# A four-layer convolution kernel: h2 of a first chunk kept in SBUF, a projection of two bands at once, and x2 stored less its group's mean

## The chip, the cores and the metric

The program runs on one core of a Trainium2 chip, in fp32 throughout. The metric is device time in microseconds. All engines work from queues of their own: PE multiplies matrices (PEld loads its weights), DVE, ACT and POOL work on 128 partitions elementwise, SP and the others issue DMAs, and instructions wait for one another by semaphores.

## What is computed

The input x is [4, 384, 64, 64]: batch B = 4, channels C = 384, which the kernel holds as three chunks (j = 0, 1, 2) of 128 partitions. Four residual layers follow each other, each on the group-normalized input:

```python
x = x + L0(gn(x))   # attention on 96 channels, then a 384 x 384 projection
x = x + L1(gn(x))   # 384 x 384, an 8 x 8 block filter, a 3 x 3 depthwise convolution,
                    # g = gelu(t[:, :192]) * t[:, 192:], then w_out: 192 -> 384
x = x + L2(gn(x))   # 3 x 3 and 5 x 5 depthwise convolutions, gates, a channel mixer
                    # h1 = gelu(bn(w1 tok)): 384 -> 768, h2 = bn(w2 h1): 768 -> 384
x = x + L3(gn(x))
```

Layer 3 is a 7 x 7 depthwise convolution whose kernel depends on the image; with v = gn(x2):

```python
x_w = gelu(mean(v) @ w_avg.T + b_avg + max(v) @ w_max.T + b_max)
xr = x_w * w_mix                                  # [b, c, 7, 7]
Gx = sqrt(sum(xr * xr)); Nx = Gx / (mean_c(Gx) + eps)
kern = gamma * (xr * Nx) + beta                   # depthwise, zero padding of 3
```

So kern is a factor per (b, c) times w_mix plus a constant beta: the kernel computes the convolution with w_mix (the same for all images) and a 7 x 7 box sum, and combines them with the factors a_s and b_s when they are known.

## The kernel before

**Attention beside layer 1.** For each batch the attention runs in 64 steps. A step's scores are four matmuls with 32 rows (L715), then the exponentials (ACT, L723) and the products with v (PE, L752). Beside the steps of batch b, the generator of layer 1 for batch b - 1 is drawn on by `side_by_side`, in shares of cost that each `yield` states. The last batch's layer 1 runs alone. Layer 1 works in eight bands of eight image rows: each column tile of a band is multiplied, filtered and brought back, then the 3 x 3 taps give three accumulators acc[0..2] (192 gated channels remain: 128 in acc[1], 64 in partitions 64 to 127 of acc[2]). `band_out` projects one band, three band heights behind: per output chunk one matmul with 128 rows (L965), one with 64 (L966) into the same PSUM tile, and a DVE add to the residual (L969). What stands in the queue of an engine is settled when the program is built, by a scheduler that takes what is ready in order of emission, and what is marked `high_priority` ahead of it.

**Layers 2 and its mixer.** Depthwise convolutions are matmuls with strips: `z_` holds all channels of a chunk transposed (rows of the image along the partitions), `toep` are band matrices that DVE and POOL build as products (L1137, L1744). The F stage (3700 to 4194 us) computes h2 = w2 h1 per batch and block of 1024 columns, copies it out of PSUM (ACT, L1439), takes its statistics (DVE, L1440) and stores it to DRAM (POOL's queue), for all j. The batch norm's scale and shift (gh, g0) are known only after all batches. `z_` (128 x 17412 fp32) stands unused during F.

**Layer 3 (`phase_g`, from about 4195 us).** `x2_of(j, b)` loads h2 in quarters of 1024 columns, scales it into PSUM (ACT, L1688, 512 columns each), adds it to the residual x (DVE, L1691), takes the sum of squares (ACT, L1693) and the maximum (DVE, L1694), and stores x2. For j = 0, `to_strips` normalizes a third of the image into `y` (ACT, L1710), transposes it on PE (L1720) and copies it into `z` (ACT L1727, DVE L1725), one batch behind `x2_of`. For j = 1 and 2 x2 is read again from DRAM and `half_strips` does the same (L1649, L1653, L1658, L1660); the scales must be laid out for two half-chunks, which `pair_scales` does by small DMAs (L1628).

`conv7` convolves eight channels: it loads a piece of w_mix (L1735), builds four `toep` (L1744, every third on POOL), and runs 32 matmuls (L1757) into PSUM. For j = 0 and 1 the result goes to DRAM (`raw`, L1766); for j = 2 the rest is added (L1769) and the output is stored. Beside the convolutions of j = 0, x2 for j = 1 and 2 is computed; then `factors` gives a_s and b_s; `boxes` (L1788 to L1851) forms the 7 x 7 box sums of each x2, combines x2, the box sum and, for j < 2, the raw convolution (L1837, L1847), and stores the output.

In this version x2 stands as it is: the group's mean gm enters where it is read, as a bias in L1649 and L1710, as the fill value and as the offsets -7 gm and -6 gm of the box sums (L1793, L1812 to L1823). The padding of the normalized image is zero, so the padding of x2 would be gm.

Of the kernel before, what the change touches and what calls it, by code (L numbers as in the profile page):

```python
# [21 lines left out]
F32 = mybir.dt.float32  # L22
# [138 lines left out]
def _layout(i):  # L161
# [38 lines left out]
    w_out_t[64:, 1] = w_out[P:]  # L200
# [26 lines left out]
class _Builder:  # L227
# [301 lines left out]
    def side_by_side(self, b, steps, others):  # L529

        per_step = ((176 if b else 0) + (42 if b + 1 < B else 0)) / 64
        ahead = 0.0
        for n, _ in enumerate(steps):
            while others is not None and ahead < n * per_step:
                piece = next(others, None)
                if piece is None:
                    others = None
                else:
                    ahead += piece
        for _ in others or ():  # L540
            pass
# [255 lines left out]
    def layer1(self, b):  # L797
# [9 lines left out]
        for n in range(-2, 4 * 11):  # L807
# [35 lines left out]
            if w == 0 and h > 2:  # L843
                k = h - 3
                yield from self.band_out(b, acc.pop(k), k, st)
# [80 lines left out]
    def band_taps(self, h, alone, acc):  # L926
# [9 lines left out]
        for j in range(NJ):  # L936
            acc.append(self.wk("acc", "acc", 5))
# [16 lines left out]
            if j == 2:  # L954
                nc.scalar.activation(acc[0][64:P], acc[2][0:64], AF.Gelu)
                nc.vector.tensor_mul(acc[2][64:P], acc[2][64:P], acc[0][64:P])
            yield

    def band_out(self, b, acc, h, st):

        nc = self.nc
        x = self.block("xa_out", self.xa[b], h, "xo", 2)
        for o in range(NJ):
            m = self.pa("out_m1") if b == B - 1 else self.pm("out_m")
            nc.tensor.matmul(m, lhsT=self.w_out[:, 0, o * P : (o + 1) * P], rhs=acc[1], start=True, stop=False)  # L965
            nc.tensor.matmul(  # L966
                m, lhsT=self.w_out[64:P, 1, o * P : (o + 1) * P], rhs=acc[2][64:P], start=False, stop=True
            )
            nc.vector.tensor_add(x[:, o], x[:, o], m)  # L969
            yield 2.0  # L970
        self.stats(st, x, h)
        nc.gpsimd.dma_start(self.x1[b][:, :, h * 512 : (h + 1) * 512], x)
# [5 lines left out]
    def open_strips(self, ctx):  # L978

        pool = ctx.enter_context(self.tc.tile_pool(name="strips", bufs=1, side="right"))  # L980
# [3 lines left out]
        self.nc.gpsimd.memset(self.z_[:, P * 132 : P * 132 + 4], 0.0)  # L984

# [317 lines left out]
    def phase_ef(self, strips):  # L1303
        tc, nc = self.tc, self.nc
        with ExitStack() as ctx:
# [110 lines left out]
            for b in range(B):  # L1416
                for i in range(4):
# [9 lines left out]
                    for j in range(NJ):  # L1427
                        out = io.tile([P, 1024], F32, tag="x", name="f_h2")
# [12 lines left out]
                        nc.gpsimd.dma_start(self.h2[b][:, j, blk], out)  # L1441
# [18 lines left out]
    def phase_g(self):  # L1460
# [8 lines left out]
        with ExitStack() as ctx:  # L1469
# [26 lines left out]
            self.s_s, self.s_b = (cp.tile([P, NJ, B], F32, tag=k, name=k) for k in ("s_s", "s_b"))  # L1496
            self.a_pair = cp.tile([P, NJ, 2, 2, 2], F32, tag="a_pair", name="a_pair")

            self.gm = cp.tile([P, NJ, B], F32, tag="gm", name="gm")
            self.off = cp.tile([P, NJ, B, 3], F32, tag="off", name="off")  # L1500
# [3 lines left out]
            self.z = self.z_[:, 0 : P * 136].rearrange("p (c k b) -> p c k b", k=34, b=B)  # L1504
            nc.gpsimd.memset(self.z_[:, P * 136 :], 0.0)
            nc.gpsimd.memset(self.z[:, :, 0], 0.0)
            self.group_means()
            behind = iter(())
            for b in range(B):
                for x in self.x2_of(0, b):  # L1510
                    next(behind, None)
                for _ in behind:
                    pass
                behind = self.to_strips(0, b, x)
            for _ in behind:
                pass
            self.pair_scales(1)
# [10 lines left out]
            for j in range(NJ):  # L1528
# [12 lines left out]
                if j == 0:  # L1541
# [3 lines left out]
                    self.pair_scales(2)  # L1545
# [5 lines left out]
    def group_means(self):  # L1551
# [4 lines left out]
        for i, k in enumerate((-6.0, -7.0, 2.0)):  # L1556
            nc.vector.tensor_scalar(self.off[:, :, :, i], self.gm, k, None, ALU.mult)
        nc.gpsimd.memset(self.s_s, 1.0)
        nc.vector.tensor_scalar(self.s_b, self.gm, -1.0, None, ALU.mult)
# [12 lines left out]
    def factors(self):  # L1572
# [3 lines left out]
        d, avg, mx = tile_of("g_d"), tile_of("g_avg"), tile_of("g_max")  # L1576
        nc.vector.tensor_sub(avg, self.mean2, self.gm)
# [9 lines left out]
        nc.vector.tensor_sub(mx, mx, self.gm)  # L1587
# [32 lines left out]
        nc.vector.tensor_copy(self.s_s[:, 2], self.a_s[:, 2])  # L1620
        nc.vector.scalar_tensor_tensor(self.s_b[:, 2], self.gm[:, 2], -1.0, self.a_s[:, 2], ALU.mult, ALU.mult)

    def pair_scales(self, j):

        for half in range(2):
            for u in range(2):
                for k, v in enumerate((self.s_s, self.s_b)):
                    self.nc.gpsimd.dma_start(  # L1628
                        self.a_pair[64 * u : 64 * u + 64, j, k, half],
                        v[64 * half : 64 * half + 64, j, u::2],  # L1630
                    )

    def half_strips(self, j, half):

        nc = self.nc
        for pair in range(2):
            for part in range(3):
# [10 lines left out]
                s, b = (self.a_pair[:, j, k, half, pair : pair + 1] for k in range(2))  # L1648
                nc.scalar.activation(y[:, inside], y[:, inside], AF.Identity, bias=b, scale=s)  # L1649
                for i, (k0, n) in enumerate(((0, 4), (4, 4), (8, 3))):  # L1650
# [6 lines left out]
                    if i == 1:  # L1657
                        nc.vector.tensor_copy(zv.rearrange("p c k b -> p k b c"), mv)  # L1658
                    else:
                        nc.scalar.copy(zv, mv.rearrange("p k b c -> p c k b"))  # L1660
# [10 lines left out]
    def x2_of(self, j, b):  # L1671

        nc = self.nc
# [6 lines left out]
        for q in range(4):  # L1680
            sl = slice(q * 1024, (q + 1) * 1024)

            h = self.gw_p.tile([P, 1024], F32, tag="w7", name="g_h2", bufs=3)
            nc.sync.dma_start(h, self.h2[b][:, j, sl])
            for v in range(2):
                m = self.pm("x2_m")
                part = slice(q * 1024 + v * 512, q * 1024 + v * 512 + 512)
                nc.scalar.activation(  # L1688
                    m, h[:, v * 512 : v * 512 + 512], AF.Identity, bias=at(self.g0), scale=at(self.gh)
                )  # L1690
                nc.vector.tensor_add(x[:, part], x[:, part], m)  # L1691
# [3 lines left out]
            yield None  # L1695
# [3 lines left out]
    def to_strips(self, j, b, x):  # L1699
# [3 lines left out]
        for part in range(3):  # L1703
            y = self.gt_p.tile([P, 11 * P], F32, tag="y", name="ax2", bufs=2)
            lo, hi = (22 * part - 1) * W, (22 * part + 21) * W
            if part == 0:
                nc.gpsimd.memset(y[:, 0:W], 0.0)
            if part == 2:
                nc.gpsimd.memset(y[:, N - lo :], 0.0)
            nc.scalar.activation(  # L1710
                y[:, max(lo, 0) - lo : min(hi, N) - lo],
                x[:, max(lo, 0) : min(hi, N)],
                AF.Identity,
                bias=self.s_b[:, j, b : b + 1],
                scale=self.s_s[:, j, b : b + 1],
            )
            for i, (k0, n) in enumerate(((0, 4), (4, 4), (8, 3))):
                m = self.pm("strip_m")
                for k in range(n):
# [166 lines left out]
```

## Time and profile before

| | us |
|---|---|
| median of 3 runs (4963.12 to 4970.23) | 4968.51 |
| the profiled execution | 4966.63 |
| its span in the profile, mean clock 0.962 | 4964.9 |
| attention, beside layer 1 of the batch before | 0 to about 2270 |
| layer 1 of the last batch alone | to about 2540 |
| layer 2's convolutions | 2543 to 3180 |
| mixer, first product | 3200 to 3690 |
| mixer, second product (F) | 3700 to 4194 |
| layer 3: head, until its first convolution matmul | 4195 to 4289 |
| layer 3: j = 0, and x2 of j = 1, 2 | 4289 to 4490 |
| layer 3: j = 1, 2 and the boxes | 4490 to 4965 |

The profile is that of one execution. A row of the groups gives line, engine, operation, result and operands with the tile's form and the number of instructions; then busy time, mean duration of one in ns, and the engine's idle time ahead of them with what ended it. A matmul in fp32 counts twice, since it runs in two passes. In the page's second part each digit is a fortieth of the span. In tables by stretch, the columns are the engines' busy time (and number of instructions), the granted clock of PE, the DMA engines' busy share, and GB/s.

### The profile page before, as it was taken

Reading aid. Unit: us, or ns where it says so; the run is one execution under the profiler, and the core shown is the slowest. Engines: PE = TensorE matmul, PEld = TensorE weight load, DVE = VectorE, ACT = ScalarE, POOL = GpSimd, SP = SyncE. Lnnn points to the kernel's source line nnn. Section 1 sums busy time; section 2 is a strip of 40 time slices with the busy share of each in tenths; the row PEclk is TensorE's granted clock in tenths of the full one; section 3 lists DMA queues with packets and bytes.
Section 4 is the critical chain, followed back from the end, with each engine's and each line's share of the span. In section 5 each row is a group of like instructions: output and inputs, shape, how many; then the busy total and the mean of one; then the engine's idle time right before and its main releaser. Section 6 shows DMA issues by size and latency. Waiting matters only on the chain.

```text
span 4964.9 us, 47732 instructions
## 1 busy us (share of the span) xinstructions
PE 4552.7 (92%) x17665; PEld 2564.5 (52%) x17665; DVE 2769.8 (56%) x4438; ACT 2136.4 (43%) x2873; POOL 777.5 (16%) x593
## 2 busy tenths in 40 slices
PE   5999999999999999998989999699999998677988
PEld 2343444434443344444557888444444443577888
DVE  5322465644666445555867778655531112667898
ACT  4444344454444444444435666411123333764321
POOL 1000000000000000000025555100000001125554
PEclk9999999999999999998989999799999999699999
DMA  5210211211111111112338999776664443896776
GB/s 169 73 47 30 85 54 55 72 56 39 64 64 51 55 45 58 58 57 78 120 122 276 291 292 292 250 278 256 256 245 157 153 152 132 316 343 203 239 255 227
DMA packets 346710, 752.64 MB, mean 152 GB/s; under 512 B 22779, under 2 KB 173158, under 8 KB 337510
## 3 DMA queue, kind: packets, MB, share of 16 engines
q1 hardware_dynamic: 280728, 475.46, 30.1%
q0 software_dynamic: 32640, 151.28, 7.9%
q10 hardware_dynamic: 33102, 122.77, 6.3%
q8 instruction: 143, 2.34, 0.2%
q14 instruction: 97, 0.79, 0.0%
HBM read 447.16 MB, written 302.25 MB: 151 GB/s over the span
## 4 chain that ended last, share of the span: by engine, by line
PE 45%; DVE 9%; DMA 4%; ACT 3%; issue 3%; POOL 1%; SPq 0%; ACTq 0%; DVEq 0%; POOLq 0%
PE h_s L1380 10%; PE h_m L1432 10%; PE conv_m L1156 9%; PE av L752 3%; PE t_m L871 2%; PE conv_m L1757 2%; DVE acc L948 2%; DMA wmix<-in_mix_t 1%; DMA g_h<-h 1%; PE out_m L966 1%; PE proj_m L785 1%; PE sc_s L715 1%; DVE toep L1744 1%; PE taps_m L941 1%; DVE toep L1137 1%
## 5 line engine op out<-in xcount | busy, mean ns | idle before, releaser
L752 PE MATMUL av<-probs,vt 128*128 128x512 f32 x2048 | 965.6, 607 | 0.0
L723 ACT ACTIVATE probs<-sc_s 128x1024 f32<-128x1024 f32 x512 | 500.9, 1021 | 789.8 <-PE av L752 783.7
L752 PEld LDWEIGHTS av<-probs,vt 128*128 128x128 f32 x2048 | 371.7, 192 | 468.1 <-issue 461.0
L1156 PE MATMUL conv_m<-toep,z 128*128 128x256 f32 x2304 | 519.4, 385 | 10.6 <-DVE toep L1137 5.1
L948 DVE SCALAR_TENSOR_TENSOR acc<-band,vecs,acc 128x512 f32<-128x512 f32 x708 | 496.9, 747 | 45.7 <-POOL band L909 39.9
L1432 PE MATMUL h_m<-f_h,cm_w_t 128*128 128x512 f32 x1152 | 496.7, 595 | 8.7 <-ACT f_h L1422 8.7
L1156 PEld LDWEIGHTS conv_m<-toep,z 128*128 128x128 f32 x2304 | 439.4, 193 | 71.0 <-DVE z L1089 4.9
L1757 PE MATMUL conv_m<-toep,z 128*128 128x128 f32 x3072 | 392.8, 286 | 42.1 <-DVE toep L1744 19.2
L1757 PEld LDWEIGHTS conv_m<-toep,z 128*128 128x128 f32 x3072 | 378.7, 202 | 44.4 <-POOL toep L1744 18.2
L1380 PE MATMUL h_s<-e_tok,cm_w_t 128*128 128x512 f32 x768 | 363.4, 596 | 5.5 <-DVE e_tok L1365 5.5
L1137 POOL TENSOR_TENSOR toep<-w,band 128x1536 f32<-128x1536 f32 x94 | 324.0, 3447 | 278.0 <-PE conv_m L1156 232.0
L1432 PEld LDWEIGHTS h_m<-f_h,cm_w_t 128*128 128x128 f32 x1152 | 220.0, 191 | 285.4 <-issue 273.3
L715 PE MATMUL sc_s<-q,k 32*128 32x512 f32 x2048 | 296.3, 647 | 21.9 <-ACT probs L723 21.4
L1440 DVE BATCH_NORM_STATS2 h_st<-f_h 128x6 f32<-128x512 f32 x96 | 66.4, 694 | 429.1 <-ACT f_h L1439 429.1
L871 PE MATMUL t_m<-w_in_t,xb 128*128 128x384 f32 x768 | 276.7, 495 | 3.4 <-DVE coef L888 2.1
L1387 ACT COPY e_h<-h_s 128x1024 f32<-128x1024 f32 x96 | 97.2, 1012 | 401.5 <-PE h_s L1380 401.5
L785 PE MATMUL proj_m<-xm,w_proj_t 128*128 128x512 f32 x576 | 265.2, 599 | 4.6 <-DVE xm L738 3.5
L792 DVE SCALAR_TENSOR_TENSOR x_res<-proj_m,bn_c,x_res 128x512 f32<-128x512 f32 x96 | 71.8, 748 | 319.0 <-PE proj_m L785 315.9
L1380 PEld LDWEIGHTS h_s<-e_tok,cm_w_t 128*128 128x128 f32 x768 | 147.0, 192 | 189.5 <-issue 183.2
L1389 DVE BATCH_NORM_STATS2 h_st<-e_h 128x6 f32<-128x512 f32 x192 | 123.4, 685 | 202.8 <-ACT e_h L1387 202.8
L871 PEld LDWEIGHTS t_m<-w_in_t,xb 128*128 128x128 f32 x768 | 142.9, 192 | 139.0 <-issue 59.3
L1380 PE MATMUL h_s<-z,cm_w_t 128*128 128x512 f32 x384 | 196.2, 593 | 0.0
(380 smaller groups left out, 6206.2 us busy)
## 6 DMA issues: line engine op xcount, KB each, us to landing
d<-d_o ACTq DMA_DIRECT2D x96, 512.0 KB
c_d<-d SPq DMA_DIRECT2D x96, 512.0 KB
hid<-e_h ACTq DMA_DIRECT2D x16, 3072.0 KB
f_h<-hid SPq DMA_DIRECT2D x16, 3072.0 KB
x_in<-in_x SPq DMA_DIRECT2D x96, 256.0 KB
x_res<-in_x SPq DMA_DIRECT2D x32, 768.0 KB
xa<-x_res POOLq DMA_DIRECT2D x32, 768.0 KB, 3.9
xa_in<-xa SPq DMA_DIRECT2D x32, 768.0 KB
```

Of the source, the lines that this page charges most:

```text
L715: nc.tensor.matmul(s[:, g], lhsT=k4[32 * g : 32 * g + 32, c], rhs=q[i][32 * g : 32 * g + 32], start=True, stop=True,)
L723: nc.scalar.activation(p[:, h * 1024 : (h + 1) * 1024], s[:, 2 * h : 2 * h + 2].rearrange("p a b -> p (a b)"), AF.Exp, scale=0.25,)
L752: nc.tensor.matmul(av, lhsT=vt[:, 4 * c + v, :], rhs=p[:, v * 512 : (v + 1) * 512], start=c == 0 and v == 0, stop=c == 7 and v == 3,)
L785: nc.tensor.matmul(m, lhsT=self.w_proj[:, j, o * P : (o + 1) * P], rhs=xm[:, j], start=j == 0, stop=j == NJ - 1,)
L871: nc.tensor.matmul(m[:, 0:C], lhsT=xb[:, j], rhs=self.w_in[:, j, :], start=j == 0, stop=j == NJ - 1,)
L948: nc.vector.scalar_tensor_tensor(out, src(j, k), w, done, ALU.mult, ALU.add)
L1137: eng.tensor_tensor(t, self.w53[:, at : at + 192].rearrange("p (m n) -> p m n", n=8).unsqueeze(2).to_broadcast([P, 24, 8, 8]), band.rearra ...
L1156: nc.tensor.matmul(m[:, c * 256 : (c + 1) * 256], lhsT=self.z_[:, at : at + P], rhs=t[:, 12 * c + 4 * i : 12 * c + 4 * i + 4].rearrange("p ...
L1380: nc.tensor.matmul(s[:, v, :], lhsT=w1[:, j, o * P : (o + 1) * P], rhs=t[j][:, v * 512 : (v + 1) * 512], start=j == 0, stop=j == NJ - 1,)
L1389: nc.vector.bn_stats(st[:, o, 8 * b + 2 * i + v, :], h[:, o, v * 512 : (v + 1) * 512])
L1432: nc.tensor.matmul(m, lhsT=w2[:, o, j * P : (j + 1) * P], rhs=h[:, o, v * 512 : (v + 1) * 512], start=o == 0, stop=o == 5,)
L1757: nc.tensor.matmul(m[:, ch * P : (ch + 1) * P], lhsT=self.z_[:, at : at + P], rhs=t[:, 8 * c + 2 * i : 8 * c + 2 * i + 2].rearrange("p m a ...
```

## The change

Four things are changed.

1. Layer 1's projection takes two bands at a time (`bands_out`). The gated 64 channels of odd bands are written to partitions 0 to 63 of acc[2], and the weights w_out_t[:, 1] lie in both halves of the partitions. Per output chunk the two 128-row matmuls come first, then the two 64-row matmuls under `high_priority`. Six `acc` buffers stand for five; `side_by_side` counts 166 for 176.
2. In F, h2 of j = 0 for batches 0 to 2 is copied into `z_` and stays there. `x2_of` works on it in place, in operations of 1024 columns and without PSUM (L1697, L1698 in the new numbering). The order of layer 3's head becomes: x2 of batches 0 to 2, strips of batch 0, then strips of batches 1 and 2 with two quarters of batch 3 ahead of each, then batch 3's rest and strips.
3. x2 is stored less its group's mean: gm is subtracted from the shift g0, so that the padding is 0, `strips7` transposes x directly with two small edge tiles, and the offsets fall away. For the output gm is added again by ACT (at the end for j = 2, with the scaled raw convolution for j < 2). `pair_scales` is only for j = 2, and the strip copies of `half_strips` are all on ACT.
4. `conv7` uses a piece of w_mix that was asked for one call earlier (`mix_of`).

```diff
-    w_out_t[64:, 1] = w_out[P:]
+    w_out_t[:64, 1] = w_out_t[64:, 1] = w_out[P:]
...
-            if w == 0 and h > 2:
-                k = h - 3
-                yield from self.band_out(b, acc.pop(k), k, st)
+            if w == 0 and h > 3 and h % 2 == 0:
+                k = h - 4
+                yield from self.bands_out(b, (acc.pop(k), acc.pop(k + 1)), k, st)
...
-                nc.vector.tensor_mul(acc[2][64:P], acc[2][64:P], acc[0][64:P])
+                at = slice(0, 64) if h % 2 else slice(64, P)
+                nc.vector.tensor_mul(acc[2][at], acc[2][64:P], acc[0][64:P])
...
+    def bands_out(self, b, accs, h, st):
+        tc, nc = self.tc, self.nc
+        xs = [self.block("xa_out", self.xa[b], h + i, "xo", 2) for i in range(2)]
         for o in range(NJ):
+            ms = [self.pa("out_m1") if b == B - 1 else self.pm("out_m") for _ in range(2)]
+            to = slice(o * P, (o + 1) * P)
+            for m, acc in zip(ms, accs):
+                nc.tensor.matmul(m, lhsT=self.w_out[:, 0, to], rhs=acc[1], start=True, stop=False)
+            with tc.high_priority():
+                for i, (m, acc) in enumerate(zip(ms, accs)):
+                    at = slice(0, 64) if i else slice(64, P)
+                    nc.tensor.matmul(m, lhsT=self.w_out[at, 1, to], rhs=acc[2][at], start=False, stop=True)
+            for m, x in zip(ms, xs):
+                nc.vector.tensor_add(x[:, o], x[:, o], m)
+            yield 3.2
...
+        self.h2_keep = [self.z_[:, b * N : (b + 1) * N] for b in range(B - 1)]
...
-                        out = io.tile([P, 1024], F32, tag="x", name="f_h2")
+                        keep = j == 0 and b < B - 1
+                        out = self.h2_keep[b][:, blk] if keep else io.tile([P, 1024], F32, tag="x", name="f_h2")
...
-                        nc.gpsimd.dma_start(self.h2[b][:, j, blk], out)
+                        if not keep:
+                            nc.gpsimd.dma_start(self.h2[b][:, j, blk], out)
...
+            self.group_means()
+            x = [None] * B
+            for b in range(B - 1):
+                for x[b] in self.x2_of(0, b):
+                    pass
             nc.gpsimd.memset(self.z_[:, P * 136 :], 0.0)
             nc.gpsimd.memset(self.z[:, :, 0], 0.0)
-            self.group_means()
-            behind = iter(())
-            for b in range(B):
-                for x in self.x2_of(0, b):
-                    next(behind, None)
-                for _ in behind:
-                    pass
-                behind = self.to_strips(0, b, x)
-            for _ in behind:
+            self.strips7(0, x[0])
+            last = self.x2_of(0, B - 1)
+            for b in range(1, B - 1):
+                next(last)
+                next(last)
+                self.strips7(b, x[b])
+            for x[B - 1] in last:
                 pass
-            self.pair_scales(1)
+            self.strips7(B - 1, x[B - 1])
+            self.mix_of(0)
...
+        nc.vector.tensor_sub(self.avg, self.mean2, self.gm)
+        nc.vector.tensor_sub(self.g0, self.g0, self.gm)
+        nc.vector.tensor_scalar(self.neg2, self.avg, -1.0, None, ALU.mult)
...
-                s, b = (self.a_pair[:, j, k, half, pair : pair + 1] for k in range(2))
-                nc.scalar.activation(y[:, inside], y[:, inside], AF.Identity, bias=b, scale=s)
+                if j == NJ - 1:
+                    nc.scalar.activation(
+                        y[:, inside], y[:, inside], AF.Copy, scale=self.a_pair[:, half, pair : pair + 1]
+                    )
...
-                    if i == 1:
-                        nc.vector.tensor_copy(zv.rearrange("p c k b -> p k b c"), mv)
-                    else:
-                        nc.scalar.copy(zv, mv.rearrange("p k b c -> p c k b"))
+                    nc.scalar.copy(zv, mv.rearrange("p k b c -> p c k b"))
...
-            for v in range(2):
-                m = self.pm("x2_m")
-                part = slice(q * 1024 + v * 512, q * 1024 + v * 512 + 512)
-                nc.scalar.activation(
-                    m, h[:, v * 512 : v * 512 + 512], AF.Identity, bias=at(self.g0), scale=at(self.gh)
-                )
-                nc.vector.tensor_add(x[:, part], x[:, part], m)
+            if j == 0 and b < B - 1:
+                h = self.h2_keep[b][:, sl]
+            else:
+                h = self.gw_p.tile([P, 1024], F32, tag="w7", name="g_h2", bufs=3)
+                nc.sync.dma_start(h, self.h2[b][:, j, sl])
+            nc.scalar.activation(h, h, AF.Identity, bias=at(self.g0), scale=at(self.gh))
+            nc.vector.tensor_add(x[:, sl], x[:, sl], h)
...
+    def strips7(self, b, x):
+        edges = self.gt_p.tile([P, 11 * P], F32, tag="y", name="edges", bufs=2)[:, 0 : 2 * P]
+        nc.gpsimd.memset(edges, 0.0)
+        nc.gpsimd.tensor_copy(edges[:, W:P], x[:, 0:W])
+        nc.gpsimd.tensor_copy(edges[:, P : P + W], x[:, N - W :])
+        for k0 in range(0, 33, 4):
+            n = min(4, 33 - k0)
+            m = self.pm("strip_m")
...
+            if k0 % 8:
+                nc.vector.tensor_copy(zv.rearrange("p c k -> p k c"), mv)
+            else:
+                nc.scalar.copy(zv, mv.rearrange("p k c -> p c k"))
...
+        wmix = self.mix_ahead
+        self.mix_of(16 * j + c0 // 8 + 1)
...
-            nc.vector.scalar_tensor_tensor(
-                hv[:, 2:8, 0], pairs_of(x, r0, 6)[:, :, 1], off(7), t[:, 2:8], ALU.add, ALU.add
-            )
+            nc.vector.tensor_add(hv[:, 2:8, 0], pairs_of(x, r0, 6)[:, :, 1], t[:, 2:8])
...
+                if j == NJ - 1:
+                    nc.scalar.activation(xq, xq, AF.Identity, bias=self.gm[:, j, b : b + 1])
...
-                nc.vector.scalar_tensor_tensor(xp, d, self.a_s[:, j, b : b + 1], xp, ALU.mult, ALU.add)
+                nc.scalar.activation(
+                    d, d, AF.Identity, bias=self.gm[:, j, b : b + 1], scale=self.a_s[:, j, b : b + 1]
+                )
+                nc.vector.tensor_add(xp, xp, d)
```

## The prediction

> **What bounds the kernel now.** I read the page's busy shares first, then the busy time of the engines by stretch, then the rows by line, then the waits of the last stage.
>
> ```profile
> PE 4552.7 (92%) x17665; PEld 2564.5 (52%) x17665; DVE 2769.8 (56%) x4438; ACT 2136.4 (43%) x2873; POOL 777.5 (16%) x593
> PEclk9999999999999999998989999799999999699999
> ```
>
> PE is busy 92% of the span at nearly full clock, so up to about 4194 us a saving counts only where it is PE's. The stretches (start:end, length, then PE, PEld, DVE, ACT, POOL busy, granted clock, DMA share, GB/s) show where that ends:
>
> ```profile
> 1000.00:2000.00 1000.00, 968.96 (x3241) 426.79 (x3239) 534.00 (x920) 470.63 (x574) 35.15 (x66) 0.98 0.16 54
> 3700.00:4194.00 494.00, 493.64 (x1149) 218.55 (x1148) 69.83 (x106) 159.88 (x189) 24.99 (x47) 1.00 0.42 156
> 4220.00:4240.00 20.00, 9.24 (x33) 5.81 (x33) 13.38 (x16) 19.68 (x26) 0.90 (x3) 0.50 0.89 329
> 4240.00:4260.00 20.00, 9.53 (x36) 6.57 (x37) 13.95 (x17) 19.81 (x27) 1.31 (x4) 0.50 0.86 322
> 4310.00:4330.00 20.00, 17.02 (x153) 16.86 (x152) 13.78 (x15) 9.22 (x15) 5.74 (x4) 1.00 0.98 372
> 4400.00:4450.00 50.00, 36.47 (x284) 35.57 (x283) 32.04 (x35) 32.45 (x47) 13.15 (x9) 0.90 0.97 332
> 4710.00:4950.00 240.00, 207.30 (x1708) 201.76 (x1707) 228.99 (x237) 53.88 (x109) 116.15 (x71) 0.96 0.72 243
> ```
>
> Four regimes: attention beside layer 1 and the h2 matmuls are PE's; layer 3's head (4205 to 4289) is ACT's, 19.7 of 20 us; its first chunk (4289 to 4490) is the DMA's at 0.97; its last part is DVE's, 229 of 240. The rows that I price with (busy us, mean ns of one):
>
> ```profile
> L966 PE MATMUL out_m<-acc,w_out_t 64*128 64x512 f32 x192 | 109.8, 660 | 13.3 <-DVE acc L956 13.3
> L1688 ACT ACTIVATE x_m<-g_h,g,gh 128x512 f32<-128x512 f32 x96 | 71.3, 773 | 59.8 <-DMA g_h<-h 50.0 <-DVE x L1691 8.7 <-DVE z L1658 1.0
> L1693 ACT ACTIVATE g_h<-x,neg 128x1024 f32<-128x1024 f32 x48 | 54.7, 1140 | 9.3 <-DVE x L1691 9.3
> L1694 DVE TENSOR_REDUCE x_max<-x 128x1 f32<-128x1024 f32 x48 | 58.0, 1209 | 0.2
> L1809 DVE TENSOR_TENSOR box<-box,box 128x512 f32<-128x512 f32 x48 | 56.6, 1185 | 14.7 <-POOL box L1808 14.7
> L1658 DVE COPY z<-strip_m 128x512 f32<-128x512 f32 x24 | 26.1, 1088 | 7.4 <-PE strip_m L1653 7.4
> L1710 ACT ACTIVATE ax<-x,s_b,s_s 128x1344 f32<-128x1344 f32 x8 | 11.9, 1492 | 0.0
> ```
>
> From the waits between 4289 and 4490 (us in total, times, longest), and then the timeline (start, us) of one score group of attention behind a projection:
>
> ```profile
> POOL toep L1744 <- DMA wmix<-in_mix_t: 53.2, 6, 15.1
> ACT x_m L1688 <- DMA g_h<-h: 46.0, 12, 8.8
> ```
>
> ```profile
> 1046.46 1.12 PE L966 MATMUL out_m<-acc,w_out_t 64*128 64x512 f32 x2
> 1047.51 1.14 PE L715 MATMUL sc_s<-q,k 32*128 32x512 f32 x8
> ```
>
> An fp32 matmul is two passes. The eight passes of four 32-row score matmuls fit into 1.14 us: the four run together. L966, with 64 rows, takes 1.05 us alone.
>
> **What the Trainium skill says.** "TensorE: Matmul & The Clock Gate", Part 3, The mechanism: matmuls on different row groups overlap, and matmuls stay in strict order. The trace agrees: in single records the four scores start within 20 ns. "TensorEngine Tiling (Array Packing)", Key Properties: changing the tiling mode drains TensorE; the trace agrees, as the scores above start 1.05 us after L966 although L966 leaves rows 0 to 63 free. "GPSIMD Engine Reference", Specifications: GpSimd shares SBUF interfaces with VectorE instructions that read two SBUF inputs. It agrees: L1809 takes 0.686 us with POOL idle, up to 2.83 beside POOL's products.
>
> **Projection of two bands.** The second matmul of band k uses rows 64 to 127 and that of band k+1 rows 0 to 63. Adjacent in PE's queue they could run together: 48 pairs x 1.05 = 50 us less. But only the second matmuls carry the high priority. In the built program's order on PE I find first(0), second(0), first(1), second(1): one pair of 48 stands adjacent with disjoint rows. Gain: 1 us. And a second matmul with high priority is placed ahead of normal ones: in 23 of 256 score groups it stands after the first of the four (before: all 256 whole). Such a group runs as 1 + 3, so 23 x 1.03 (one group's spacing) = 24 us more of PE work, where PE is 97% busy and ACT waits for it. Bounds: 15 if a third falls into PE's 3% of idle time, 28 with a switch of tile size (0.09) each. For the last batch alone, bands 6 and 7 come out together after band 7's taps: before, the last adds end 7 us after the last tap (2524.7 to 2531.9); three more matmul pairs of 1.9 us and one band's statistics come behind, half beside DVE: +3 (0 to +6). The sixth acc buffer and 166 for 176 steps (24 x 2.0 against 12 x 3.2 units) move nothing that PE waits for. Sum: +27.
>
> **Kept h2.** Twelve stores of 512 KB leave the F stage, where DMA is at 0.42 and PE at 493.6 of 494: nothing. The first ones of layer 3 need no load: L1688 waited 2.64 us for it, until 4208.45; the first in-place activation can start after 4205.8. Per quarter ACT now has 1.17 (estimate from L1693's 1.14 for the same size) + 1.14 + 0.19 for the sum read = 2.5 us; DVE an add (~1.2) and a reduction 1.21 = 2.4. Twelve quarters on ACT: 30 us, to 4236. Only then are the kept values dead and may strips be written there: this serializes what was interleaved before, 12 quarters first, then 27 strip groups. A group's four transposes cost 0.86 us at the clock of 0.5 seen there (single records start 0.214 us apart), its copy 0.84 to 1.12 on ACT or 1.09 on DVE, five and four per batch. Against before, ACT loses per batch three scalings (L1710, 1.5 each). The fourth batch's x needs x[0]'s buffer: free at about 4242, 2 MB at 330 GB/s lands near 4250; its four quarters and last nine groups are 13 us of DVE behind that. Convolution starts at 4267 to 4271 instead of 4289.06: -20 us at the head. A late x[3] would make this 4280.
>
> What follows is DMA bound, so the head's gain counts only as far as bytes come earlier; what is late next is the queue. From the stretches (length x GB/s), 12 MB move between 4205 and 4242 and 82 MB from there to 4490. After, 6 MB of h2 loads are gone and I count 8 MB moved by 4242 (three x2 stores of 2 MB, 2 MB of prefetches): 12 + 82 - 6 - 8 = 80 MB are left, 231 us at this stage's mean of 347 GB/s. Until convolution starts the queue lacks requests for 0 to 6 us, 3 taken: 4242 + 234 = 4476 against 4490, **-14** (bounds: +3 if 5 MB fewer move early, -22 if the whole head's gain stays). Loading wmix a chunk ahead removes POOL's 53 us of waits but no bytes; with the DMA full I count nothing more for it. L1691, which read PSUM, becomes an add of two SBUF tensors that must wait for POOL's 2.4 us products: 32 in this stage, up to 2.4 each, where DVE is busy 134 of 200 us; hidden as long as the DMA decides.
>
> **Mean taken out of x2.** x2 is now less its group's mean, so 0 is the padding. In the last 475 us DVE is busy 413. Removed there: 18 of the strip copies L1658 x 1.09 = 20, now on ACT, which has under 9 of 20 us; 24 small ones (L1812, L1823), about 6; 132 box adds without a scalar operand x 0.055 (difference of such rows) = 7; L1847 as a plain add, 2. Together -33 on DVE, some 23 of them in the part where DVE decides. New on ACT: 32 bias passes of 0.7 and 32 scalings of 1.2, 61 us, beside its idle half; they lie in the chain PSUM, DVE, ACT, store, but the store only follows. The new adds wait for POOL. The end is set by the convolution's stream (PE to 4957), so I take **-15** (bounds -5, where PE's 28 us of idle time limits it, and -25). Scale DMAs on POOL's queue fall from 16 to 4: they stand in the chain for 3.2 us at 4509: -2.
>
> **Sum.** +27 - 14 - 15 - 2 = -4. The profiled execution took 4966.63 (span 4964.9), so 4962.6; the median of the runs shown is 2 us above that execution. I say 4963.
>
> **Rivals.** (a) Slower: the DMA queue takes the head's gain back. Place: 4205 to 4242, where the in-place activations ask for nothing; each MB not moved there costs 2.9 us later. With 3 MB moved instead of 8 the first stage ends at 4491 and the whole is 4966.6 + 27 + 1 - 17 = 4978, with the box stage's gain at its lower bound 4988. It decides from there, since 10 us above before needs all of the head's gain gone. For it: a DMA share of 0.97 after 4310. Against: the stores are in the same queue, and x and h2 of the later chunks may load as soon as buffers are free. (b) Clearly faster: head -22, box stage -25, splits 15 to 20 because part falls into PE's idle 3%: 4936 to 4945. For it: DVE at 229 of 240 with 33 us less to do. (c) The pairs do run together: 50 less, 4913. Against: the order on PE, which leaves one pair adjacent.
>
> **How the numbers follow.** The forecast with its neighbourhood (4953 to 4973) gets 0.44, (a) 0.26, (b) 0.22, (c) 0.03, the gap between forecast and (a) 0.05. A difference under 0.2%, 10 us, can't be told from none. Faster by more, below 4958.6: (b), (c) and 0.15 of the forecast = 0.40. Within: 0.29 + 0.05 = 0.34. Slower: 0.26. Range 4930 to 4993: it leaves out (c) and the tails of (a) and (b).
>
> **What would show it.** Right: 23 score groups split, and attention ending some 24 us later; convolution starting 18 to 22 us sooner after the head's begin than before (then 84 us); DMA share still near 1 to the end of that stage; DVE below 390 in the last part. Wrong: second matmuls starting within 20 ns of each other in most pairs; the head not shorter than 75 us; DVE's adds above 1.7 us on average.

## The result, and the profile after

The kernel after took 4970.38 us in the median of 4 runs (4966.19 to 4979.35), the kernel before 4966.11 beside it: ratio 1.001, 95% interval 0.9993 to 1.0028. Measured again with more runs (`e5_after_again`, 13 runs against 35), the ratio is 1.0017, interval 1.0009 to 1.0025: no change, or 4 to 12 us slower. The profiled execution spans 4964.1 us. So the sum of the forecast, -4 us, was off by some 10 us; the table shows that two of its terms were off by more. It is made from the times at which matmuls start in the trace: last product of attention, last projection of layer 1, last conv of layer 2, last h2 matmul, first 7 x 7 convolution, the gate's first and last matmul (from there the factors a_s, b_s are known), last convolution, end.

| stretch, us | before | after | after again | forecast of the difference |
|---|---|---|---|---|
| attention, to its last product | 2253.5 | 2265.4 | 2272.1 | +24 |
| layer 1 of the last batch alone | 277.3 | 285.0 | 286.6 | +3 |
| layer 2's convolutions | 611.2 | 615.4 | 615.7 | 0 |
| mixer, both products | 1051.1 | 1052.1 | 1054.2 | 0 |
| head of layer 3 | 96.0 | 74.2 | 73.6 | -20 |
| x2 part: first convolution to the gate | 202.9 | 187.0 | 187.9 | +6 |
| gate | 3.9 | 3.9 | 3.9 | 0 |
| box part: gate to the last convolution | 461.8 | 475.1 | 470.9 | -17 |
| rest | 7.2 | 6.2 | 6.2 | 0 |

Single executions differ: attention ended between 2265 and 2282 us in the ten profiles below that share its instructions with the kernel after (median 2272.6), and layer 2's convolutions, which the change doesn't touch, took 611 to 624. One profile decides no smaller difference there. Layer 3's head, 73.6 to 75.8 us in the twelve profiles that leave its code as it is, is far steadier.

The gate's matmuls stand in PE's queue among the convolutions, so how many convolution passes stand ahead of them shifts time between x2 part and box part. It is 1152 before and 1140 in both profiles of the kernel after, close enough to compare; where an experiment moves it, the time from the first to the last convolution compares better: 668.6 us before, 666.0 and 662.7 after. Over both parts together the change thus won 3 to 6 us.

The page's busy times of the kernel after:

```profile
PE 4580.6 (92%) x17665; PEld 2583.1 (52%) x17665; DVE 2719.8 (55%) x4341; ACT 2150.1 (43%) x2881; POOL 779.3 (16%) x596
```

PE has the same 17665 instructions as before and 28 us more to do; DVE has 50 us less, ACT 14 more. Where PE's come from is seen in the rows of the groups, kernel after:

```profile
L715 PE MATMUL sc_s<-q,k 32*128 32x512 f32 x2048 | 323.0, 649 | 21.5 <-ACT probs L723 21.3
L974 PE MATMUL out_m<-acc,w_out_t 64*128 64x512 f32 x192 | 112.3, 676 | 2.0 <-DVE acc L958 2.0
```

The scores, untouched by the diff, were busy 296.3 us before and are 323.0 now. L974, once L966, is at 112.3 (109.8): the pairs save nothing. The timeline of PE in the kernel after (start, us) shows both:

```profile
741.95 1.13 PE L970 MATMUL out_m<-acc,w_out_t 128*128 128x512 f32 x2
743.01 1.12 PE L715 MATMUL sc_s<-q,k 32*128 32x512 f32 x2
744.06 1.12 PE L974 MATMUL out_m<-acc,w_out_t 64*128 64x512 f32 x2
745.11 1.13 PE L715 MATMUL sc_s<-q,k 32*128 32x512 f32 x6
```

One score matmul takes as long as the other three together, because a second matmul stands between them; the trace has 23 such groups.

The stretches of layer 3, the kernel before first, then the kernel after; columns as in the forecast. Each set is head, x2 part, rest:

```profile
4205.00:4289.00 84.00, 35.58 (x132) 23.91 (x132) 56.46 (x66) 79.15 (x105) 7.96 (x17) 0.50 0.85 308
4289.00:4490.00 201.00, 152.18 (x1217) 149.61 (x1218) 134.40 (x150) 117.94 (x170) 64.27 (x39) 0.89 0.95 335
4490.00:4965.00 475.00, 403.62 (x3330) 391.01 (x3328) 412.74 (x461) 138.15 (x260) 240.32 (x163) 0.96 0.69 225
```

```profile
4230.00:4292.00 62.00, 23.41 (x132) 19.69 (x132) 56.26 (x52) 56.88 (x71) 9.73 (x17) 0.64 0.68 262
4292.00:4477.00 185.00, 150.17 (x1204) 147.21 (x1205) 132.41 (x113) 100.61 (x135) 60.39 (x35) 0.91 0.98 355
4477.00:4964.00 487.00, 416.82 (x3344) 407.92 (x3342) 361.53 (x417) 195.34 (x340) 251.89 (x186) 0.92 0.70 230
```

In the head ACT's work fell from 79 to 57 us, and ACT and DVE are each busy in 56 to 57 of these 62 us. In the x2 part the DMA moved 355 GB/s instead of 335. In the rest DVE's work fell by 51 us and the stretch grew. The box part alone, before, after and after again:

```profile
4495.90:4957.70 461.80, 397.47 (x3278) 385.22 (x3278) 411.18 (x457) 134.22 (x255) 240.30 (x162) 0.96 0.69 226
4482.90:4958.00 475.10, 410.71 (x3290) 402.00 (x3290) 358.60 (x413) 192.51 (x336) 247.16 (x183) 0.92 0.69 227
4494.00:4964.90 470.90, 401.31 (x3290) 391.63 (x3290) 359.90 (x413) 191.99 (x336) 247.89 (x183) 0.95 0.70 229
```

In the first profile after, PE's nearly same work took 13 us more at a lower clock (0.92 for 0.96); in the second it took 4 us more, at 0.95.

### The profile page after: what moved, and what is told of

The parts are those of the page before. It is cut to its first block, busy times and chain, and to the rows that moved or that the text cites. A ratio compares the mean times of both kernels' runs of the same rounds, so it can differ in the third digit from the quotient of the medians.

```text
span 4964.1 us, 47555 instructions
## 1 busy us (share of the span) xinstructions
PE 4580.6 (92%) x17665; PEld 2583.1 (52%) x17665; DVE 2719.8 (55%) x4341; ACT 2150.1 (43%) x2881; POOL 779.3 (16%) x596
## 5 line engine op out<-in xcount | busy, mean ns | idle before, releaser
L715 PE MATMUL sc_s<-q,k 32*128 32x512 f32 x2048 | 323.0, 649 | 21.5 <-ACT probs L723 21.3
L1451 DVE BATCH_NORM_STATS2 h_st<-f_h 128x6 f32<-128x512 f32 x72 | 49.8, 693 | 319.3 <-ACT f_h L1450 319.3
L715 PEld LDWEIGHTS sc_s<-q,k 32*128 32x128 f32 x2048 | 88.5, 185 | 216.0 <-ACT probs L723 137.4
```

Source lines behind the costliest of these rows:

```text
L715: nc.tensor.matmul(s[:, g], lhsT=k4[32 * g : 32 * g + 32, c], rhs=q[i][32 * g : 32 * g + 32], start=True, stop=True,)
```

## Experiments

All are edits of the kernel after and were timed in five rounds against the kernel before on the same chip, which is what the ratios refer to.

**1. What the projection costs: `e1_old_projection`, `e2_pairs_adjacent`.** The first puts the old one-band projection back:

```diff
-            if w == 0 and h > 3 and h % 2 == 0:
-                k = h - 4
-                yield from self.bands_out(b, (acc.pop(k), acc.pop(k + 1)), k, st)
+            if w == 0 and h > 2:
+                k = h - 3
+                yield from self.band_out(b, acc.pop(k), k, st)
```

The second keeps two bands and mends the order:

```diff
-            for m, acc in zip(ms, accs):
-                nc.tensor.matmul(m, lhsT=self.w_out[:, 0, to], rhs=acc[1], ...)
-            with tc.high_priority():
+            for m, acc in zip(ms, accs):
+                first = nc.tensor.matmul(m, lhsT=self.w_out[:, 0, to], rhs=acc[1], ...)
+            with tc.high_priority(), tc.high_priority(offset=100), tc.issue_after(first.ins):
```

Both second matmuls are queued behind both first ones, and ahead of the scores rather than level with them. In the kernel after, `high_priority` starts the count of priorities anew for the scores and for the second matmuls, so that the second one (number 1) goes between the scores number 0 and 1; the order in the timeline above fits this.

> The kernel after, with layer 1's projection one band at a time as before (old loop over bands, old share of 176, five acc buffers). Theory: the two-band projection costs 20 to 25 us, because 23 score groups run as 1 + 3 and the last batch's end is drawn out; so this runs at 4944 to 4950, attention's last product at about 2253 and the layer's last projection at about 2531 us, and everything behind keeps the times of the kernel after relative to it. Rival: the two-band projection costs nothing of its own and the later start is the spread of single executions; then this is within 5 us of the kernel after, 4966 to 4975.

Measured: 4949.78 us, ratio 0.9954 (0.9939 to 0.9969). Attention ends at 2248.9, the last batch takes 276.5. The scores are back at 295.1 us. So the two-band projection as it was queued costs 21 to 31 us.

> The kernel after, with the second matmuls of both bands queued behind both first ones and ahead of all else, so that 43 of 48 pairs stand next to each other on PE and all 256 score groups are whole. Theory: 64-row matmuls on disjoint rows run together, each pair 1.05 us shorter: about 45 us less PE work in the pairs and 24 us less in the score groups, together 55 to 70 us, 4900 to 4915; in the trace the two second matmuls of a pair start within 20 ns. Rival: they do not run together (the same PSUM or weight path holds the second up); then only the 24 us of the score groups return, 4945 to 4950, and the second starts 1.05 us behind.

Measured: 4914.75 us, ratio 0.9882 (0.9865 to 0.99); attention ends at 2208.6. The groups' rows and a stretch of PE's timeline in this run:

```profile
L715 PE MATMUL sc_s<-q,k 32*128 32x512 f32 x2048 | 298.1, 651 | 22.2 <-ACT probs L723 22.0
L974 PE MATMUL out_m<-acc,w_out_t 64*128 64x512 f32 x192 | 63.9, 676 | 5.6 <-DVE acc L958 5.6
```

```profile
736.30 1.13 PE L974 MATMUL out_m<-acc,w_out_t 64*128 64x512 f32 x4
737.36 3.70 PE L752 MATMUL av<-probs,vt 128*128 128x512 f32 x8
```

All four passes of the pair lie in 1.13 us, where each matmul took 1.12 alone (43 pairs stand so, their starts 7 ns apart, and all 256 score groups are whole); L974 falls from 112.3 to 63.9 us and the scores return to 298.1. That is 73 us of PE work, and 56 to 67 us of time against the kernel after (by the medians of the two first runs, and by the ratios with its second). So the pairing works on this chip, and the change's order kept it from happening.

**2. What shortens head and x2 part: `e6_no_keep`, `e4_own_mix_load`, `e12_x2_psum`.** Three parts are undone singly: h2 of the first chunk is stored and loaded again; w_mix is loaded in the call that uses it; x2 of chunks 1 and 2 is formed in halves through PSUM.

```diff
-                        keep = j == 0 and b < B - 1
+                        keep = False
...
-            if j == 0 and b < B - 1:
+            if False:
```

> The kernel after, with h2 of the first chunk stored and loaded as for the other chunks; the order of the head and the in-place operations of 1024 columns stay. Theory: the head (after 74 to 76 us) was won by not loading h2 and by leaving out the scalings L1710; without the kept h2 the 12 loads of 512 KB return, the head is some 8 to 15 us longer, and the x2 part behind is as the kernel after's or up to 5 us longer: total 4975 to 4990. Rival: the head is set by ACT's and DVE's work in both, so the loads hide and the total stays within 5 us of the kernel after.

Measured: 4999.13 us, ratio 1.0052 (1.0039 to 1.0064), some 18 us more than the kernel after. The head takes 86.3 us, 12.5 more, in line with the theory; of the 22 us that the head won, the kept h2 is more than half. The busy ACT and DVE (60 and 62 of 86 us) no longer fill it:

```profile
4244.00:4330.10 86.10, 33.94 (x147) 26.32 (x146) 62.19 (x89) 60.14 (x76) 8.29 (x20) 0.57 0.80 297
```

The x2 part is 193.5. The profiled execution is the slowest of five (5016.16), so its other stretches say less.

```diff
-            self.mix_of(0)
...
-        wmix = self.mix_ahead
-        self.mix_of(16 * j + c0 // 8 + 1)
+        self.mix_of(16 * j + c0 // 8)
+        wmix = self.mix_ahead
```

> The kernel after, with each piece of w_mix loaded in the call that uses it, as before. Theory: x2's part of layer 3 ended 16 us sooner behind the head's gain because toep builders no longer stand waiting for w_mix and the DMA queue is full from the first convolution on; without it that part (first convolution to the factors, 187 us after, 203 before) is 8 to 16 us longer, the total 4972 to 4985. Rival, as predicted blind: the DMA bytes bound it, so the load's place gives at most 3 us.

Measured: 4984.7 us, ratio 1.002 (1.001 to 1.0031). Its median is 14 us above the kernel after's first and 6 above its second, but the ratios' intervals overlap. The x2 part (190.1) did not grow, against the theory. What grew is the time until the second chunk's convolutions start, 185.7 us after the first chunk's against 169.5 and 170.5. The gate stands behind 1044 convolution passes instead of 1140, and the box part, with the others to do, is 483.6. But this is the slowest of the run's 13 executions (4996.72). So if the load ahead has a worth, it lies in the convolutions and not in the x2 part; the times don't show that it has one.

```diff
-            nc.scalar.activation(h, h, AF.Identity, bias=at(self.g0), scale=at(self.gh))
-            nc.vector.tensor_add(x[:, sl], x[:, sl], h)
+            if j == 0:
+                nc.scalar.activation(h, h, AF.Identity, bias=at(self.g0), scale=at(self.gh))
+                nc.vector.tensor_add(x[:, sl], x[:, sl], h)
+            else:
+                for v in range(2):
+                    m = self.pm("x2_m")
+                    part = slice(q * 1024 + v * 512, q * 1024 + v * 512 + 512)
+                    nc.scalar.activation(m, h[:, v * 512 : v * 512 + 512], AF.Identity, bias=at(self.g0), scale=at(self.gh))
+                    nc.vector.tensor_add(x[:, part], x[:, part], m)
```

> The kernel after, with x2 of the second and third chunk formed as before: two scalings of 512 columns into PSUM and two DVE additions from PSUM, in place of one of each of 1024 columns in SBUF. All else stays, the head too. Theory: the x2 part (first convolution to the factors, 187 to 191 us after, 203 before) is set by the DMA queue, which is full there from the first convolution on and has fewer bytes left; so it stays at 186 to 192. Rival: the longer operations in SBUF free the load buffers sooner and so keep the queue full; then it goes back to 197 to 203.

Measured: 4987.84 us, ratio 1.0041 (1.0027 to 1.0054), and the x2 part takes 206.1 us: my theory fell, and the time lies 3 us above the rival's range. Part of it is the gate's place, behind 1186 convolution passes instead of 1140; the box part is 463.2, and from first to last convolution it is 676.6 us, 11 to 14 more than the kernel after. So the form of these operations has a worth. The waits of SP's queue in the x2 part (us in total, times, longest) are, for the kernel before, the kernel after, and this run:

```profile
SPq L1684 <- ACT g_h L1693: 107.5, 27, 15.7
SPq L1735 <- DVE toep L1744: 12.1, 4, 7.7
```

```profile
SPq L1696 <- ACT g_h L1700: 61.4, 20, 10.0
SPq L1733 <- DVE toep L1749: 51.9, 15, 6.2
```

```profile
SPq L1696 <- ACT g_h L1709: 90.0, 25, 10.7
SPq L1742 <- DVE toep L1758: 41.9, 12, 11.5
```

The load of the next h2 waits in SP's queue until ACT is done with a buffer. This wait fell by 46 us with the change, and 29 of them come back here. In the same queue the loads of w_mix, now asked for earlier, wait 40 us more for buffers than before. The rival's reason, that a buffer comes free sooner, is not shown: from a quarter's first scaling to the end of its squares it takes 6.6 us on average in the kernel before, 6.1 in the kernel after and 6.2 here, although two scalings of 773 ns became one of 1237. Which step of the longer way makes the wait is open.

**3. What lengthens the box part: `e3_raw_on_dve`, `e7_raw_early`, `e8_dve_strips`, `e9b_bias_first`, `e10b_no_mean_added`.** The waits of the kernel after between gate and last convolution name a new one, ACT's L1845 for the load of raw:

```profile
PE box_m L1831 <- ACT ht L1827: 53.2, 22, 6.8
ACT in_raw L1845 <- DMA in_raw<-raw: 53.0, 17, 6.3
```

Before, DVE read raw, and waited 1.2 us for it in all; PE waited 35.7 us for `ht`:

```profile
PE box_m L1835 <- ACT ht L1831: 35.7, 22, 5.3
```

In ACT's queue the `ht` copies stand behind L1845, and PE's box matmuls behind those. But all of PE's waits in the part add up to 64.2 us before and 64.3 after (69.5 in the second profile), so this way of the loss was a theory to be tested.

```diff
-                if j == NJ - 1:
+                if True:
                     nc.scalar.activation(xq, xq, AF.Identity, bias=self.gm[:, j, b : b + 1])
...
-                nc.scalar.activation(
-                    d, d, AF.Identity, bias=self.gm[:, j, b : b + 1], scale=self.a_s[:, j, b : b + 1]
-                )
-                nc.vector.tensor_add(xp, xp, d)
+                nc.vector.scalar_tensor_tensor(xp, d, self.a_s[:, j, b : b + 1], xp, ALU.mult, ALU.add)
```

> The kernel after, with the raw convolution scaled and added by one DVE operation, as before, and the group's mean added by ACT to each 512 columns for all chunks. ACT then waits for no load of raw. Theory: in the last part ACT waits 53 us for raw, ahead of the ht copies that PE's box matmuls need[...]; without it PE waits under 35 us for ht (53 after, 36 before) and the part behind the factors shortens by 8 to 15 us: 4955 to 4962. Rival: DVE's load bounds that part anyway (this gives DVE some 6 us more): within 4 us of the kernel after.

Measured: 4970.92 us, ratio 0.9996 (0.9988 to 1.0003), below the second measurement of the kernel after, with intervals that don't overlap. The box part takes 462.2 us, 9 to 13 less, as the theory said; in the five profiles that leave this part's code and the gate's place as they are it lies between 470.7 and 479.7. ACT has no less to do (197.7 us, 192.5 in the kernel after), so it is not the amount of its work. But PE's wait for `ht` is 47.9 us rather than under 35: the gain is there, the way that the theory gave it is not confirmed.

> The kernel after, once more, as the measure for the other three of this job: 4966 to 4975. Between the end of the h2 matmuls and the first convolution 74 to 76 us, from there to the factors 187 to 191, from there to the last convolution matmul 470 to 476.

This is the measure beside the next three: 4978.93 us, 4 us above the range expected for it; the stretches are as expected (73.6, 187.9 and 470.9 us).

> The kernel after, with each piece of raw asked for at the beginning of its part of the box sums, not at its end; ACT scales it as in the kernel after. Theory: the wait for the load at the head of ACT's queue (53 us) is what lengthens the last part; it falls below 15 us, and the part from the factors to the last convolution shortens from 475 to about 462 us as it did with the sum on DVE. Rival: it is ACT's additional 40 us of work, not the wait, that delays the ht copies: the part stays at 470 to 476 although the wait goes. A buffer of rest held longer could make the convolutions wait, which would show as PE or ACT waiting for rest.

The edit moves the two statements that allocate `d` and load raw into it from the end of the part to its beginning. Measured: 4986.76 us, ratio 1.0037 (1.0024 to 1.005), box part 479.1. It tells neither case apart, as the wait did not go (63.1 us): the load now waits in SP's queue for one of three buffers, 91.2 us, and holds up what is behind it.

> The kernel after, with every third strip copy of half_strips on DVE again, as before (24 copies of 1.09 us, 18 of them behind the factors). Blind step: DVE bounds the last part, so 20 us of DVE work make it 10 us or more longer, 480 to 486 us. Theory now: DVE is no bound there (359 of 475 us busy) and ACT's queue is; the part is the same or up to 6 us shorter, 466 to 475.

```diff
-                    nc.scalar.copy(zv, mv.rearrange("p k b c -> p c k b"))
+                    if i == 1:
+                        nc.vector.tensor_copy(zv.rearrange("p c k b -> p k b c"), mv)
+                    else:
+                        nc.scalar.copy(zv, mv.rearrange("p k b c -> p c k b"))
```

Measured: 4976.38 us, ratio 1.0007 (1.0 to 1.0015). The box part is 465.4, with 386.8 us of DVE work against 359.9: more work for DVE, and no longer. The x2 part grew to 196.5, so that from first to last convolution the run takes 666.9 us, as the kernel after (666.0 and 662.7).

> The kernel with raw scaled and added by DVE (as in the run before with raw on DVE), but ACT adds the group's mean to x ahead of the box matmuls' result, so that ACT neither waits for raw nor for DVE's box additions ahead of its next ht copy. Theory: what the last part lost is ACT's queue standing behind waiting instructions; ACT's work is the same here (32 more passes than the kernel after, 32 fewer scalings). From the factors to the last convolution 450 to 460 us (471 to 475 in the kernel after, 462 with raw on DVE). Rival: 462 or more, because the convolution stream on PE, not the box chain, sets that part, and it was DVE's wait for raw alone.

The edit is shown against e3's kernel, with raw on DVE:

```diff
+                xq = x[:, (2 * part + q) * 512 : (2 * part + q + 1) * 512]
+                nc.scalar.activation(xq, xq, AF.Identity, bias=self.gm[:, j, b : b + 1])
                 m = self.pm("ht_m")
...
                 nc.vector.scalar_tensor_tensor(xq, m, scale, xq, ALU.mult, ALU.add)
-                if True:
-                    nc.scalar.activation(xq, xq, AF.Identity, bias=self.gm[:, j, b : b + 1])
```

Measured: 4970.36 us, ratio 0.9997 (0.9986 to 1.0007), box part 465.1: the rival. PE's wait for `ht` is back at its value of before, and the part is no shorter than e3's:

```profile
PE box_m L1833 <- ACT ht L1829: 36.9, 22, 4.1
```

> As the run with raw on DVE, but the group's mean is not added to the output at all: it leaves out 96 passes of ACT, about 69 us of its work, and the waits ahead of them. Theory: as with the mean added first, 450 to 460 us from the factors to the last convolution, a few us less than that run if ACT's work counts besides its waits. Rival: DVE's saving of 33 us is worth nothing in that part because PE and POOL set it; then 460 to 464, as before and with raw on DVE.

Of the diff just shown only the two removed lines are made, again on e3's kernel. Measured: 4964.26 us, ratio 0.9987 (0.998 to 0.9994), box part 459.8, where the two expectations meet. The busy times of that part (window, length, PE, PEld, DVE, ACT, POOL, clock, DMA share, GB/s):

```profile
4496.80:4956.60 459.80, 403.78 (x3291) 394.15 (x3290) 363.37 (x413) 135.45 (x272) 246.71 (x183) 0.94 0.72 234
```

ACT has as much to do as before (134.2 us in 461.8), DVE 48 us less (411.2), and the part is 2 us shorter. So DVE's saving is worth little there: 2 us, in profiles that differ by some 5 us when repeated, and PE's work took 6 us more at a clock of 0.94 for 0.96. PE with 404 busy and 37.6 waiting for `ht` accounts for most of the part; which of its work would shorten it was not tried.

**4. Both mends: `e11b_best`.** e2's order, raw on DVE and the bias first.

> The two mends together: pairs of second matmuls adjacent and score groups whole, raw on DVE, the mean added ahead of the box matmuls. Theory: the gains add, 56 us of the pairs and 10 to 20 us of the last part: 4895 to 4906. Rival: the last part's gain is lost in the end of the program, 4910 to 4918.

Measured: 4906.12 us in the median of 4 runs (4902.47 to 4919.43), ratio 0.9872 (0.9858 to 0.9886): the fastest of all, 1.3% below the kernel before. It lies at the upper end of the theory, but against e2 (0.9882) the second mend is not told apart; the profiled execution, the slowest of the four, has 470.4 us in the box part.

## Why the forecast came out as it did

**Projection: right in mechanism and size.** 23 groups split, L715 27 us busier (24 forecast); one band at a time again is 21 us faster by the first medians, 31 by the ratios of the second (27 forecast). Of the terms, attention gives about 21 us (the median of the ten profiles less the mean of the two with one band), the last batch 8 to 9, not 3. That term was mis-sized: at its end PE's clock is 0.50 (2543 to 2551 us), and a pair of matmuls takes 4.0 us there where 1.9 was counted; the kernel before shows 4.0 too, for its last pair at 2527.75. From DVE's last product to the last addition 11.9 us pass (7.2 before). Rival (c) was rightly put down by the order, and e2 shows that only the order stood against it.

**Kept h2: head right, its follow-up wrong.** The head won 22 us (20). Then I counted 80 MB to be moved from 4242 until the gate, at 347 GB/s, and gave 6 us back. The x2 part instead won 15 to 16. The stretch from that point on (49 us behind the last h2 matmul) to the gate, before and after:

```profile
4242.00:4490.00 248.00, 177.43 (x1312) 166.99 (x1313) 165.19 (x185) 164.04 (x228) 66.24 (x47) 0.82 0.94 332
4266.80:4479.00 212.20, 167.85 (x1317) 161.94 (x1315) 154.71 (x136) 123.85 (x162) 64.73 (x42) 0.90 0.96 348
```

The rate was right, 348 GB/s. The step that failed is the byte count, "12 + 82 - 6 - 8 = 80 MB are left": 348 GB/s over 212.2 us is 74 MB, and 6 MB less are 18 us at this rate. From the last h2 matmul to the gate the traffic fell from 95.2 to 84.6 MB, where I took off only the 6 of h2. (Between 4205 and 4242 it was 10.7 MB before, not 12.) The count held everything that the queue moved for needed by the gate. Of two 2 MB loads for the boxes, which the gate does not need, the second was asked for 17.6 us ahead of the gate before and 2.8 us ahead of it after; where the rest of the difference lies was not traced. The last load of h2, which the gate does need, was asked for 27 us ahead of it before and 20 after. A DMA share of 0.97 said that the queue was full; it did not say that what was in it was needed. e12 shows that the new form of the x2 operations is part of the gain, 11 to 14 us over both parts, though I had priced it only as a risk ("L1691 ... becomes an add of two SBUF tensors"); by which way is open. The risk itself, that these adds wait for POOL, did not show: one of 1024 columns took 1.37 us on average, as much as two of 512 before. (The longest L1809 that the forecast read as 2.83 us took 2.87.)

**Mean taken out: wrong sign.** Forecast -17 with the scale DMAs, measured +9 to +13. Two steps failed. The forecast's "part where DVE decides" took a busy share of 95% for the bound: DVE's work fell by 53 us (33 forecast, though the terms listed add up to 35), and 48 us less gained 2 us (e10b), 27 us more cost nothing over the convolutions' stretch (e8). And the new ACT work was said to lie "beside its idle half ... the store only follows". The wait for raw, which came into ACT's queue with it (53 us), was priced at nothing. e3, which moves this wait back to DVE, wins the 9 to 13 us back with ACT as busy. That the `ht` copies behind it carry the loss to PE is not shown: e9b brings PE's wait for them to 36.9 us, as before, and gains nothing over e3. Rival (a) priced the slower side by the DMA of the head; what came was another queue, ACT's. The four signs of being right came about, more or less (23 groups split and attention about 21 us later, the convolution 22 us sooner, a DMA share of 0.98, DVE at 361 in the last part), and none of them tested whether less DVE work makes the last part shorter.

That the result was inside the range is luck: the x2 part's surplus of some 21 us and the box part's deficit of 26 to 30 nearly cancelled.

## What to carry to other kernels

Before work is given to an engine with idle time, ask what it will wait for and what stands behind it in that engine's queue; here a wait for a load, moved to an engine that was busy in 192 of 475 us, cost 9 to 13 us. A full DMA queue is a bound only for what is needed: count the bytes that must land before the next step, not all that the queue moves until then. A busy share near 1 names a candidate for the bound, and only taking work away shows whether it is one. When instructions must run side by side, look at their order in the queue: a priority that sets them level with others can drive both groups apart. And where one instruction in a queue marks the border of two parts, compare the time over both.

## What was not expected of the hardware

Two fp32 matmuls with 64 rows each and disjoint rows, back to back, take 1.13 us together, as one does alone (1.12), although they write different PSUM tiles of all 128 partitions and load different weights. Adjacent in the queue is what it took: 43 pairs in e2 start 7 ns apart, where the kernel after, with a score matmul or another projection between them, gives each its own 1.12 us. The same box matmuls and convolutions cost PE 411 us at a mean clock of 0.92 and 401 at 0.95, in two executions of one program; what sets the clock there was not tried.
